# A row LSTM's three-tap filter as F(2,3) on pixel pairs, with the normalisation of x moved to GpSimd

## The chip, the cores and the metric

The kernel runs on one core of a Trainium2 chip. The metric is the time of one launch in device microseconds (us). The kernel before took 2895.79 us, the median of 3 runs (2895.6 to 2897.91). The clocks named are the mean granted clock of TensorE, with 1 as full speed.

## The reference, cut to what matters

```python
# x: (8, 96, 128, 128) float32.  GroupNorm with 32 groups, then a row LSTM, then the residual.
its = conv(gn(x), W_is * mask, taps over w)       # input part of the gates, all rows at once
def step(h, c, row):                              # 128 rows, one after the other
    ss    = conv(h, W_ss, three taps over w)      # 96 channels of h to 4*96 gate channels
    gates = ss + its[row]
    f, i, o = sigmoid(...);  g = tanh(...)
    c = f * c + i * g
    h = o * tanh(c)
    return h, c
out = x + h of every row
```

Each row needs the h of the row above, so the rows are a chain. The mask leaves two taps of the input filter (w-1 and part of w). Everything is float32.

## The kernel before

Channels lie on the partitions. The eight images are two halves of four, and one row of one half is a 512-column operand. I call the work for one row of one half a **step**; there are 2 x 128 = 256 of them, and the halves alternate, so that TensorE works on one half while ScalarE and VectorE work on the other. Four rows make a **block**, eight steps. The gates of a step are four products of 512 columns for each of three tiles of 128 gate channels. They are summed in `ps`, which the kernel places in the memory called PSUM, where all its products are written; all other tiles lie in the memory called SBUF:

```python
for a in order:                       # normalised x, channels 0-63, two taps in one product
    nc.tensor.matmul(ps[a], wt[:, 3, bass.ts(a, P)], xin[:, r, :, :], start=True, stop=False)
for a in order:
    for p in range(3):                # h at w-1, w, w+1 (taps 0 and 1 also carry x of channels 64-95)
        kk = C if p == 2 else P
        nc.tensor.matmul(ps[a], wt[0:kk, p, bass.ts(a, P)],
                         hin[0:kk, r, :, p : p + W], start=False, stop=(p == 2))
# ... (cut) tanh and sigmoid of three tiles on ScalarE; f*c, i*g, c on VectorE; tanh(c) on ScalarE
nc.vector.tensor_mul(h, sg[2], th)
nc.gpsimd.tensor_add(xr, xr, h)       # residual, in place
```

VectorE also normalises x for the block to come, one image after each step:

```python
for r in range(R):
    for s in range(NH):
        step(s, k, r)
        if k + 1 < NB:
            normalise(s, k + 1, r)    # three nc.vector.tensor_scalar(...)
```

## Time and profile before

| | before |
|---|---|
| median time | 2895.79 us |
| span of the profiled run | about 2891 us |
| TensorE busy | 2642.7 us, 91% |
| VectorE, ScalarE, GpSimd busy | 45%, 42%, 11% |
| one step | 10.32 us |

The prediction below shows the busy table, the chain, the main groups and a step of the timeline. Two more lines of the page of the kernel before matter later: the TensorE clock in 40 equal slices of the span (in tenths; 9 is 90% or more), and VectorE's larger group of normalisations (line, engine, operation, operands and shapes, count; then total busy us and mean ns; then the idle time before them).

```profile
PEclk9999999999999999999999999999999999999999
...
L163 DVE TENSOR_SCALAR x<-x,rstd,nmr 64x508 f32<-64x508 f32 (+1 forms) x512 | 327.1, 639 | 20.9 <-PE ps L185 13.7
```

The runs of this kernel have a mean clock of 0.999. These normalisations are work of VectorE that the change takes away; they lie beside TensorE's products, so they cost the kernel before nothing.

### The profile page before, as it was taken

The numbers are of one execution on the slowest core, as the hardware profiler recorded it, in microseconds if no ns is written. First come the engines' busy times: TensorE is split into PE (matmuls) and PEld (weight loads), VectorE is DVE, ScalarE is ACT, GpSimd is POOL, SyncE is SP. The second block draws the span as 40 slices with busy tenths as digits, with TensorE's granted clock in tenths as the row PEclk, the third lists the DMA queues.
The fourth block names the chain that finished last, engine by engine and source line by source line (L and its number), as shares of the span: only waits on it lengthen the run. The fifth ranks groups of instructions, "written<-read, shape, count | busy, mean of one in ns | idle before, by whom it ended". The sixth has DMA issues, their size and how long they took to land.

```text
span 2890.6 us, 18393 instructions
## 1 busy us (share of the span) xinstructions
PE 2642.7 (91%) x6148; PEld 1164.1 (40%) x6148; DVE 1313.2 (45%) x2070; ACT 1212.1 (42%) x1796; POOL 317.8 (11%) x282
## 2 busy tenths in 40 slices
PE   0007999999999999999999999999999999999998
PEld 0003444444444444444444444444444444444443
DVE  6776444443344444433444444334444443344422
ACT  0003444444444444444444444444444444444444
POOL 1000111111111111111111111111111111111111
PEclk9999999999999999999999999999999999999999
DMA  9992111001111111011111110111111101111000
GB/s 229 236 239 69 44 44 44 26 21 41 44 44 44 44 44 29 21 39 44 44 44 44 44 32 20 37 44 44 44 44 44 33 22 34 44 44 44 22 22 22
DMA packets 55597, 152.96 MB, mean 53 GB/s; under 512 B 3024, under 2 KB 3152, under 8 KB 52432
## 3 DMA queue, kind: packets, MB, share of 16 engines
q1 hardware_dynamic: 54784, 151.01, 19.8%
q10 hardware_dynamic: 720, 0.78, 0.1%
q8 instruction: 51, 0.84, 0.1%
q14 instruction: 42, 0.34, 0.0%
HBM read 101.44 MB, written 50.33 MB: 53 GB/s over the span
## 4 chain that ended last, share of the span: by engine, by line
PE 91%; DMA 6%; DVE 2%; issue 1%; ACT 0%; POOLq 0%; POOL 0%; DVEq 0%; ACTq 0%
PE ps L191 68%; PE ps L185 23%; DMA xc<-in_x_dram 6%; DVE bst L114 2%; DMA wt<-in_w_ss_dram 0%; POOLq L282 0%; POOL x L220 0%; DVE st L115 0%; DVE hb L218 0%; DVE c L214 0%; DVE ig L213 0%; ACT g L205 0%; ACT th L215 0%; PE pm L127 0%; PE pv L133 0%
## 5 line engine op out<-in xcount | busy, mean ns | idle before, releaser
L191 PE MATMUL ps<-hb,wt 128*128 128x512 f32 (+1 forms) x4608 | 2022.0, 592 | 0.0
L191 PEld LDWEIGHTS ps<-hb,wt 128*128 128x128 f32 (+1 forms) x4608 | 872.5, 189 | 1107.8 <-issue 1107.5
L205 ACT ACTIVATE g<-ps,bias 32x512 f32<-32x512 f32 x768 | 522.7, 681 | 1164.5 <-PE ps L191 1164.4
L185 PE MATMUL ps<-x,wt 128*128 128x512 f32 x1536 | 702.7, 593 | 8.1 <-issue 8.1
L212 DVE TENSOR_TENSOR fc<-sf,c 96x512 f32<-96x512 f32 x256 | 176.1, 688 | 1077.3 <-ACT sf L208 1077.3
L220 POOL TENSOR_TENSOR x<-x,hb 96x512 f32<-96x512 f32 x256 | 308.5, 1205 | 2561.2 <-DVE hb L218 2457.0
L185 PEld LDWEIGHTS ps<-x,wt 128*128 128x128 f32 x1536 | 290.8, 189 | 378.0 <-issue 377.8
L163 DVE TENSOR_SCALAR x<-x,rstd,nmr 64x508 f32<-64x508 f32 (+1 forms) x512 | 327.1, 639 | 20.9 <-PE ps L185 13.7
L213 DVE TENSOR_TENSOR ig<-si,g 96x512 f32<-96x512 f32 x256 | 176.2, 688 | 233.6 <-ACT g L205 231.7
L215 ACT ACTIVATE th<-c 96x512 f32<-96x512 f32 x256 | 161.3, 630 | 264.4 <-DVE c L214 264.4
L218 DVE TENSOR_TENSOR hb<-so,th 96x512 f32<-96x512 f32 x256 | 175.7, 686 | 161.8 <-ACT th L215 160.5
L127 PE MATMUL pm<-d,gm 96*96 96x8 f32 x2 | 0.5, 318 | 228.8 <-DVE d L125 228.8
L214 DVE TENSOR_TENSOR c<-fc,ig 96x512 f32<-96x512 f32 x256 | 175.8, 687 | 8.7
L114 DVE BATCH_NORM_STATS2 bst<-xc 96x6 f32<-96x512 f32 x256 | 154.9, 675 | 51.8 <-DMA xc<-in_x_dram 51.8
L208 ACT ACTIVATE so<-ps,bias 96x512 f32<-96x512 f32 x256 | 174.7, 683 | 6.5
L208 ACT ACTIVATE si<-ps,bias 96x512 f32<-96x512 f32 x256 | 174.7, 682 | 3.2
L208 ACT ACTIVATE sf<-ps,bias 96x512 f32<-96x512 f32 x256 | 174.6, 682 | 3.1
L163 DVE TENSOR_SCALAR hb<-x,rstd,nmr 32x512 f32<-32x512 f32 x256 | 124.1, 540 | 1.3
L135 ACT ACTIVATE t<-v 96x8 f32<-96x8 f32 x1 | 0.2, 208 | 225.1 <-DVE v L134 225.1
L127 PEld LDWEIGHTS pm<-d,gm 96*96 96x96 f32 x2 | 0.4, 256 | 228.8 <-DVE d L125 228.8
L115 DVE BATCH_NORM_AGGREGATE st<-bst 96x2 f32<-96x192 f32 x8 | 8.1, 1018 | 0.3
L102 POOL MEMSET hb<- 128x2080 f32 x4 | 7.3, 1830 | 0.0
(27 smaller groups left out, 10.2 us busy)
## 6 DMA issues: line engine op xcount, KB each, us to landing
xc<-in_x_dram SPq DMA_DIRECT2D x32, 1536.0 KB, 15.2
x<-in_x_dram SPq DMA_DIRECT2D x64, 768.0 KB, 5.0
out_dram<-x SPq DMA_DIRECT2D x64, 768.0 KB, 4.3
wt<-in_w_ss_dram ACTq DMA_DIRECT2D x1, 432.0 KB, 11.4
wt<-in_w_is_dram ACTq DMA_DIRECT2D x3, 96.0 KB, 11.1
gm<-in_gmat_dram ACTq DMA_DIRECT2D x1, 36.0 KB, 9.5
bias<-in_b_ss_dram ACTq DMA_DIRECT2D x1, 1.5 KB, 10.2
bias<-in_b_is_dram ACTq DMA_DIRECT2D x1, 1.5 KB, 9.8
```

What stands on the lines that cost most here:

```text
L114: nc.vector.bn_stats(bst[:, k * (CH // SN) + j, :], xc[:, bass.ts(j, SN)])
L163: nc.vector.tensor_scalar(dst, t[lo:hi, j, :, 0:w], rstd[lo:hi, b : b + 1], nmr[lo:hi, b : b + 1], ALU.mult, ALU.add,)
L185: nc.tensor.matmul(ps[a], wt[:, 3, bass.ts(a, P)], xin[:, r, :, :], start=True, stop=False)
L191: nc.tensor.matmul(ps[a], wt[0:kk, p, bass.ts(a, P)], hin[0:kk, r, :, p : p + W], start=False, stop=(p == 2),)
L205: nc.scalar.activation(g[a * 32 : (a + 1) * 32], ps[a][C:P], AF.Tanh, bias=bias[C:P, a : a + 1])
L208: nc.scalar.activation(sg[a], ps[a][0:C], AF.Sigmoid, bias=bias[0:C, a : a + 1])
L212: nc.vector.tensor_mul(fc, sg[0], c)
L213: nc.vector.tensor_mul(ig, sg[1], g)
L214: nc.vector.tensor_add(c, fc, ig)
L215: nc.scalar.activation(th, c, AF.Tanh)
L218: nc.vector.tensor_mul(h, sg[2], th)
L220: nc.gpsimd.tensor_add(xr, xr, h)
```

## The change

**Intent.** Take a pair of neighbouring pixels and the four values of h that their three taps touch, d0 to d3. With the filter F(2,3) the two outputs need four products in place of six:

```text
m1 = (d1+d2) * (w0+w1+w2)/2      m2 = (d2-d1) * (w0-w1+w2)/2      (the signs are the kernel's)
first output  = m1 + m2 + (d0-d2) * w0
second output = m1 - m2 + (d3-d1) * w2
```

In the cut below, `mm(a, half, w, operand)` is one product with filter `w` into half 0, half 1 or (None) both halves of tile `a`. The weights are combined once. Per step VectorE makes the sum and the difference of h (`vs`, `vf`), and GpSimd makes the other differences (`vd`). TensorE makes m1 and m2 of each tile. ScalarE copies m1 (adding the bias), VectorE writes m1+m2 and m1-m2 back into the same PSUM, and TensorE accumulates the rest on top. Products of h are now 256 columns wide. The normalisation goes to GpSimd, because VectorE has more to do. The part of x in channels 64 to 95 is shared with the products of h, so GpSimd makes its sums and differences too.

```diff
-        for a in order:
-            nc.tensor.matmul(ps[a], wt[:, 3, ...], xin[:, r, :, :], start=True, stop=False)
-        for a in order:
-            for p in range(3):
-                nc.tensor.matmul(ps[a], wt[0:kk, p, ...], hin[0:kk, r, :, p : p + W], ...)
+        for a in order:
+            mm(a, 0, 1, vs[s][i][:, r].rearrange(flat), start=True)
+            mm(a, 1, 2, vf[s][i][:, r].rearrange(flat))
+            m1 = gt(f"m{a}", (P, HB))
+            lo, hi = ps[a][:, 0:HB], ps[a][:, HB : 2 * HB]
+            nc.scalar.activation(m1, lo, AF.Identity, bias=bias[:, a : a + 1])
+            nc.vector.tensor_add(lo, m1, hi)
+            nc.vector.tensor_sub(hi, m1, hi)
+        for a in order:
+            mm(a, None, 4, xn[s][i][:, r].rearrange("p t b j -> p (t b j)"))
+            mm(a, 0, 0, vd[s][i][:, r, 1, :, 0:J])
+            mm(a, 1, 3, vd[s][i][:, r, 0, :, 0:J], stop=True)
 ... (cut: gates and cell state as before, without the bias)
+            nc.vector.tensor_add(vs[s][n][0:C, rn], e, o)
+            nc.vector.tensor_sub(vf[s][n][0:C, rn], o, e)
+            nc.gpsimd.tensor_sub(vd[s][n][0:C, rn, :, :, 0:J], strided(h...), h3)
-        nc.gpsimd.tensor_add(xr, xr, h)
+        nc.gpsimd.tensor_add(xr_, xr_, h3)
 ... (cut)
+    with tc.manual_schedule(engines={mybir.EngineType.Pool}):      # GpSimd keeps the order written
+        for k in range(NB):
 ...
+                    step(s, k, r)
+                    if k + 1 < NB:
+                        normalise_own(s, k + 1, r)               # GpSimd: tensor_scalar, memset
+                        if r > 0:
+                            normalise_shared(s, k + 1, r - 1)    # GpSimd: tensor_scalar, two sums
+                        if r == R - 1:
+                            normalise_shared(s, k + 1, r)
```

## The prediction

Terms are cut from the text below; the sums stand as my estimates:

- **VectorE.** The source of the 0.42 us of a 256-column operation is cut. A straight line between two sizes in the kernel before (163 ns for 8 columns, 687 for 512) gives 0.42 us too.
- **GpSimd.** Cut are its time for a normalisation and what rests on it: the term of the shared part of an image and the 8 us before the first product (249 + 8 = 257). The last row of a block came to 6.9 us with the cut terms; the terms that still stand (1.18 + 1.18 + 0.12) are 2.48 of it. The block wait in the 2635 and the 2876 us, and so the 2768, rests on this sum.
- **Contention.** What stands is the measured row (1.51 us), and the chances of 55% and 45%, which were my guess.

> **What bounds the kernel now.** I read the busy table first, then the chain of work that ended last, then the groups of instructions, and last the timeline of one step (a step is one image row of one batch half; there are 2 x 128 = 256).
>
> ```profile
> PE 2642.7 (91%) x6148; PEld 1164.1 (40%) x6148; DVE 1313.2 (45%) x2070; ACT 1212.1 (42%) x1796; POOL 317.8 (11%) x282
> PE 91%; DMA 6%; DVE 2%; issue 1%; ACT 0%; POOLq 0%; POOL 0%; DVEq 0%; ACTq 0%
> L191 PE MATMUL ps<-hb,wt 128*128 128x512 f32 (+1 forms) x4608 | 2022.0, 592 | 0.0
> L205 ACT ACTIVATE g<-ps,bias 32x512 f32<-32x512 f32 x768 | 522.7, 681 | 1164.5 <-PE ps L191 1164.4
> L185 PE MATMUL ps<-x,wt 128*128 128x512 f32 x1536 | 702.7, 593 | 8.1 <-issue 8.1
> L212 DVE TENSOR_TENSOR fc<-sf,c 96x512 f32<-96x512 f32 x256 | 176.1, 688 | 1077.3 <-ACT sf L208 1077.3
> L220 POOL TENSOR_TENSOR x<-x,hb 96x512 f32<-96x512 f32 x256 | 308.5, 1205 | 2561.2 <-DVE hb L218 2457.0
> ```
>
> The chain is 91% TensorE, and the matmul group L191 has 0.0 us of idle time ahead of it: the row loop is TensorE-bound without a gap. ScalarE and VectorE idle because they wait for matmuls, so their time is hidden. 6144 matmul instructions in 256 steps are 24 a step: each of the program's 12 float32 products is two instructions. The timeline shows the period and the handoffs:
>
> ```profile
> 1508.72 2.74 PE L185 MATMUL ps<-x,wt 128*128 128x512 f32 x6
> 1508.72 0.19 PEld L185 LDWEIGHTS ps<-x,wt 128*128 128x128 f32 x1 [0.24 <-issue]
> 1508.92 0.68 ACT L205 ACTIVATE g<-ps,bias 32x512 f32<-32x512 f32 x1 [1.20 <-PE ps L191]
> 1509.63 0.69 DVE L213 TENSOR_TENSOR ig<-si,g 96x512 f32<-96x512 f32 x1 [1.19 <-ACT g L205]
> 1511.14 0.63 ACT L215 ACTIVATE th<-c 96x512 f32<-96x512 f32 x1 [0.83 <-DVE c L214]
> 1511.87 0.69 DVE L218 TENSOR_TENSOR hb<-so,th 96x512 f32<-96x512 f32 x1 [0.82 <-ACT th L215]
> ...
> 1519.04 2.74 PE L185 MATMUL ps<-x,wt 128*128 128x512 f32 x6
> ```
>
> A step lasts 1519.04 - 1508.72 = 10.32 us, or 0.43 us an instruction. The next half's matmuls start at 1508.72 and this half's last tanh at 1508.92, so TensorE to ScalarE costs 0.20 us after the slot; ScalarE to VectorE about 0.03, VectorE to ScalarE 0.09, to GpSimd 0.07. 256 x 10.32 = 2642 of the 2891 us span: about 249 us are statistics, start and end.
>
> One more pair of rows matters, a normalisation (VectorE) meeting the residual add (GpSimd):
>
> ```profile
> 259.77 1.51 DVE L163 TENSOR_SCALAR hb<-x,rstd,nmr 32x512 f32<-32x512 f32 x1
> 259.82 1.18 POOL L220 TENSOR_TENSOR x<-x,hb 96x512 f32<-96x512 f32 x1 [244.19 <-DVE hb L218]
> ```
>
> This normalisation takes 0.54 us elsewhere. Here it ends 0.28 us after the GpSimd add ended (261.00): it was held for the whole add.
>
> [...]
>
> **The change part by part.**
>
> *TensorE.* A step has 15 products: three of 512 columns and twelve of 256. That is 6 x 0.43 + 24 x 0.215 = 7.74 us, three quarters of 10.32. A 0.19 us weight load still fits a 0.215 us slot, narrowly. Were TensorE the only bound: 256 x 7.74 = 1981, plus about 257 (the old 249[...]) = 2238 us.
>
> *VectorE.* Removed: (327.1+124.1)/256 = 1.76 us of normalisation a step. Added: six 256-column sums into PSUM and two for h, 8 x 0.42 = 3.4. Total 2.75 + 3.4 = 6.1 us. *ScalarE.* Three 256-column copies with bias; 0.68 less 256 columns at (681-208)/504 ns (the 8-column root took 208) is about 0.45 to 0.47. Total 4.7 + 1.4 = 6.1 us. *GpSimd.* Per step: a difference 1.18 and the residual add 1.18,[...] a memset 0.12[...]; but the last row of a four-row block has two shared parts, 6.9 us. *DMA* reads the rows about 2.3 times, roughly 117 MB beside 50 MB of stores over 2000 us: hidden.
>
> None of these sums exceeds 7.74; what counts is the new path inside a step. TensorE makes the sums and differences products of all gate tiles (2.58 us), then must wait until ScalarE and VectorE have written m1+m2 and m1-m2 back into PSUM. By the instruction order of the built program, each engine does that after work of the other half. With 0 at the end of the previous step's matmul slots: ScalarE tanh 0.20-0.88, sigmoid to 1.56, copies to 2.03 and 2.50, tanh(c) to 3.13, third copy to 3.60. VectorE i*g 0.91-1.60, c to 2.33, two sums and a difference, overlapping a little, to 3.48. So TensorE, done with its first part at 2.58, resumes at 3.56: 1 us lost. Its second part, 5.16 us, ends at 8.72, if VectorE's remaining h (3.41-4.10), difference, two sums of h, sum and difference (to about 5.9) stay ahead of the third tile's start at 7.0. They do without contention. **8.72 x 256 + 257 = 2489 us.**
>
> *Block boundary.* The first matmul of a new block waits for GpSimd's last shared part. Its queue for that step starts when h is done, 4.1 after the step's own matmuls, and lasts 6.9, to 11.0; TensorE does the other half's step meanwhile and wants it at 8.72. Some 2.3 us are lost, twice in 8 steps (both halves): 0.57 a step, 9.29 x 256 + 257 = **2635 us**.
>
> [...] h ends at 4.10, GpSimd's difference runs 4.17-5.35, and VectorE's two sums of h (two SBUF inputs) stand in the queue ahead of the third tile's PSUM sums. If the first waits to 5.35 (ends 5.63), then GpSimd's residual add goes first (to 6.67), then the second sum (6.95), the third tile is ready at 7.8 and TensorE starts it at 7.9 instead of 7.0: a step of 9.62. The boundary wait, with GpSimd held in turn by VectorE, is about 2.5: 9.62 + 0.61 = 10.23, and 256 x 10.23 + 257 = **2876 us**.
>
> **The rivals.** (A) TensorE stays the bound, about 2240 us: speaks for it that every engine's sum is below 7.74; against it the dependence ScalarE to VectorE to TensorE in mid-step, which two alternating halves cannot hide because the engines take the halves in turn. (B) GpSimd's block end and the mid-step wait, no real contention: about 2635. (C) Full exclusion[...]: about 2876, level with before; for it the 1.51 us row[...], against it [...]that two queued VectorE sums may pass together. (D) GpSimd is worse than estimated (interleaved pixels, normalisation 0.9 us) with full exclusion: each boundary wait grows by 1 to 2 us, about 3000.
>
> **Range and chances.** I give full exclusion 55% and the rest 45%: 0.55 x 2876 + 0.45 x 2635 = 2768 us. The range 2570 to 2970 spans from just above the contention-free path to most of D. Faster by 2% means under 2838: nearly all of B, a fifth to a quarter of C's spread: 0.57. Within 2%: 0.26. Slower: 0.17.
>
> **What would show it right or wrong.** In the profile after, TensorE's slots should be about 0.215 us for 256 columns[...]. The matmul of the interleaved x should carry an idle of about 1 us in each step, ended by VectorE; the third tile's should too if the lock is real, and then sums of h take 1 to 1.3 us rather than 0.42. The first matmul of each block should wait 2 to 3 us for GpSimd. GpSimd rows: [...]adds near 1.2. The prediction fails low if VectorE and GpSimd overlap freely and blocks join smoothly, and high if GpSimd's strided work is slow enough to bound each step, or if gaps lower TensorE's granted clock, which is full in all slices before.

## The result, and the profile after

The changed kernel took 2945.64 us, the median of 4 runs (2938.35 to 2952.89); the kernel before took 2895.78 us in the same rounds. The ratio is 1.0172, with a 95% interval of 1.0155 to 1.0190. A ratio is the mean time of one kernel's fast runs over that of the other's fast runs of the same rounds, so it is not quite the ratio of the medians. By the limit of 2% this is "the same", on the slower side. The profiled run spans 2936.5 us at a mean clock of 0.958.

First the page of the changed kernel: its busy table and the engines' shares of the chain that ended last.

```profile
PE 2255.3 (77%) x7688; PEld 1481.7 (50%) x7688; DVE 2074.1 (71%) x3352; ACT 1364.6 (46%) x2564; POOL 1567.7 (53%) x1828
...
DVE 46%; PE 21%; POOL 18%; DMA 5%; ACT 5%; issue 4%; ACTq 0%; POOLq 0%; DVEq 0%
```

No engine is busy for more than 77%. TensorE's share of the chain fell from 91% to 21%; VectorE and GpSimd now carry 64%. The chain goes through three of them, so this kernel is bound by handoffs. The change also loads more of x (HBM read 185.73 MB, 101.44 before), but DMA is on the chain only with the loads for the statistics at the start, 5% of it.

Next the groups of the same page, in the columns explained above.

```profile
L246 PE MATMUL ps<-xn,wt 128*128 128x512 f32 x1536 | 842.1, 630 | 250.7 <-DVE ps L260 249.4
L246 PE MATMUL ps<-vs,wt 128*128 128x256 f32 x1536 | 522.5, 425 | 212.0 <-POOL vs L231 212.0
L259 DVE TENSOR_TENSOR ps<-m,ps 128x256 f32<-128x256 f32 x768 | 309.4, 422 | 274.1 <-ACT m L258 274.1
L287 DVE TENSOR_TENSOR vf<-hh 96x256 f32<-96x256 f32 x254 | 380.7, 1499 | 0.0
L286 DVE TENSOR_TENSOR vs<-hh 96x256 f32<-96x256 f32 x254 | 294.0, 1157 | 0.0
L288 POOL TENSOR_TENSOR vd<-hh 96x512 f32<-96x512 f32 x254 | 263.7, 1038 | 1082.3 <-DVE hh L279 1082.3
L294 POOL TENSOR_TENSOR x<-x,hh 96x512 f32<-96x512 f32 x256 | 377.3, 1474 | 14.1 <-DVE hh L279 14.1
L198 POOL TENSOR_SCALAR xn<-xr,rstd,nmr 128x512 f32<-128x512 f32 x256 | 247.8, 968 | 199.0 <-DVE nmr L176 198.9
L198 POOL TENSOR_SCALAR vd<-x,rstd,nmr 32x512 f32<-32x512 f32 x256 | 235.5, 920 | 23.4
L231 POOL TENSOR_TENSOR vs<-vd 32x256 f32<-32x256 f32 x256 | 247.5, 967 | 21.3
```

Read three things here. TensorE's idle time stands before the products of `xn` (it waits for VectorE's write-back into `ps`) and before the products of `vs` (it waits for GpSimd). The write-back itself, a 256-column VectorE operation into PSUM, takes 422 ns; the sums of h, `vs` and `vf`, are as many columns and take 1157 and 1499 ns. And each of GpSimd's operations shown takes 0.92 us or more, the normalisations 0.92 to 0.97.

The timeline of the changed kernel shows both waits and a third thing (start in us, duration, engine, line, operation, operands; in brackets the idle time before it and what ended it).

```profile
1500.00 1.04 POOL L288 TENSOR_TENSOR vd<-hh 96x512 f32<-96x512 f32 x1 [5.07 <-DVE hh L279]
1500.17 1.15 DVE L286 TENSOR_TENSOR vs<-hh 96x256 f32<-96x256 f32 x1
1501.00 1.47 POOL L294 TENSOR_TENSOR x<-x,hh 96x512 f32<-96x512 f32 x1
1501.24 1.51 DVE L287 TENSOR_TENSOR vf<-hh 96x256 f32<-96x256 f32 x1
...
1503.12 0.43 DVE L260 TENSOR_TENSOR ps<-m,ps 128x256 f32<-128x256 f32 x1
1503.60 1.13 PE L246 MATMUL ps<-xn,wt 128*128 128x512 f32 x2 [0.51 <-DVE ps L260]
...
1508.72 1.22 PE L246 MATMUL ps<-vs,wt 128*128 128x256 f32 x2 [3.12 <-POOL vs L231]
...
1510.58 1.06 PE L246 MATMUL ps<-vs,wt 128*128 128x256 f32 x2
...
1519.97 0.59 PE L246 MATMUL ps<-vs,wt 128*128 128x256 f32 x2
```

- **The lock.** GpSimd's difference ends at 1500.00 + 1.04 = 1501.04, and VectorE's sum `vs` ends at 1501.32, 0.28 us later. GpSimd's residual add ends at 1502.47, and `vf` ends at 1502.75, again 0.28 us later; over all steps the medians of both are 0.28. I call this the lock: the sum, whose two inputs are both in SBUF, ends only after the GpSimd operation beside it. The write-back of the third tile stands behind them in VectorE's queue, and TensorE waits for it at 1503.60.
- **The block's end.** The first product of a new block waits 3.12 us for the last shared sums of GpSimd.
- **The clock.** After that wait the same pair of products takes 1.06 us where it takes 0.59 later. From start to start, an instruction of 256 columns takes 0.427 us instead of 0.216. Half the clock lasts for about the first ten instructions of a step (in the clock records 3.4 us, or 6.8 in 13 of 57 stretches).

I sorted the steps by their row in the block (start of the first product to start of the next step's first product, medians):

| step of the block | period before, us | period after, us |
|---|---|---|
| row 0, first half | 10.32 | 14.36 |
| row 0, second half | 10.32 | 11.10 |
| rows 1, 2 and row 3, first half | 10.32 | 9.36 |
| row 3, second half | 10.32 | 12.65 |

A regular step of 9.36 us is 7.76 us of product slots, 0.82 us at the wait for the write-back (a slot of 0.934 in place of 0.216, and 0.10 in the next one) and 0.78 us at the wait for the third tile (0.90, and again 0.10). By the means (14.16, 10.85 and 12.67) a block of eight steps takes 84.5 us, which is 8 x 9.36 = 74.9 and about 9.7 at the boundary: twice 3.3 us of waiting and twice about 1.5 us of half clock.

So the account closes: 224 us before the first product of a row and 10 after the last one, 256 x 7.76 = 1987 us of slots, 256 x 1.60 = 410 us of waits in the steps, and 31 x 9.7 = 300 us at the block boundaries give 2931 us; the span is 2936.5. The change saved 256 x (10.32 - 7.76) = 655 us of TensorE's slots and spent 710 us on waits.

### The profile page after: what moved, and what is told of

Its sections match the earlier page's. It is cut to its first block, busy times and chain, and to the rows that moved or that the text cites. A ratio compares the mean times of both kernels' runs of the same rounds, so it can differ in the third digit from the quotient of the medians.

```text
span 2936.5 us, 26168 instructions
## 1 busy us (share of the span) xinstructions
PE 2255.3 (77%) x7688; PEld 1481.7 (50%) x7688; DVE 2074.1 (71%) x3352; ACT 1364.6 (46%) x2564; POOL 1567.7 (53%) x1828
## 3 DMA queue, kind: packets, MB, share of 16 engines
q10 hardware_dynamic: 1040, 1.18, 0.2%
q8 instruction: 63, 1.03, 0.1%
HBM read 185.73 MB, written 50.33 MB: 80 GB/s over the span
## 4 chain that ended last, share of the span: by engine, by line
DVE 46%; PE 21%; POOL 18%; DMA 5%; ACT 5%; issue 4%; ACTq 0%; POOLq 0%; DVEq 0%
PE ps L246 21%; DVE vf L287 9%; DVE ps L259 8%; DVE vs L286 7%; DVE ps L260 6%; DVE hh L279 6%; DMA xc<-in_x_dram 5%; POOL vd L198 5%; DVE g L273 4%; DVE c L274 4%; POOL vs L231 4%; ACT g L269 4%; POOL x L294 3%; POOL xn L198 2%; POOL vd L288 2%
## 5 line engine op out<-in xcount | busy, mean ns | idle before, releaser
L246 PE MATMUL ps<-xn,wt 128*128 128x512 f32 x1536 | 842.1, 630 | 250.7 <-DVE ps L260 249.4
L269 ACT ACTIVATE g<-ps 32x512 f32<-32x512 f32 x768 | 454.2, 591 | 953.2 <-PE ps L246 953.1
L246 PEld LDWEIGHTS ps<-vd,wt 128*128 128x128 f32 x3072 | 582.2, 190 | 411.7 <-issue 370.6
L246 PE MATMUL ps<-vd,wt 128*128 128x256 f32 x3072 | 788.2, 378 | 0.0
L246 PE MATMUL ps<-vs,wt 128*128 128x256 f32 x1536 | 522.5, 425 | 212.0 <-POOL vs L231 212.0
L258 ACT ACTIVATE m<-ps,bias 128x256 f32<-128x256 f32 x768 | 358.0, 466 | 386.6 <-PE ps L246 385.8
L246 PE MATMUL ps<-vf,wt 128*128 128x256 f32 x1536 | 517.6, 422 | 0.0
L259 DVE TENSOR_TENSOR ps<-m,ps 128x256 f32<-128x256 f32 x768 | 309.4, 422 | 274.1 <-ACT m L258 274.1
L294 POOL TENSOR_TENSOR x<-x,hh 96x512 f32<-96x512 f32 x256 | 377.3, 1474 | 14.1 <-DVE hh L279 14.1
L287 DVE TENSOR_TENSOR vf<-hh 96x256 f32<-96x256 f32 x254 | 380.7, 1499 | 0.0
L260 DVE TENSOR_TENSOR ps<-m,ps 128x256 f32<-128x256 f32 x768 | 325.4, 424 | 8.9
L286 DVE TENSOR_TENSOR vs<-hh 96x256 f32<-96x256 f32 x254 | 294.0, 1157 | 0.0
```

The costliest lines, as they stand in the source:

```text
L246: nc.tensor.matmul(o, wt[:, p, bass.ts(a, P)], rhs, start=start, stop=stop, skip_group_check=True)
L258: nc.scalar.activation(m1, lo, AF.Identity, bias=bias[:, a : a + 1])
L259: nc.vector.tensor_add(lo, m1, hi)
L260: nc.vector.tensor_sub(hi, m1, hi)
L269: nc.scalar.activation(g[a * 32 : (a + 1) * 32], ps[a][C:P], AF.Tanh)
L286: nc.vector.tensor_add(vs[s][n][0:C, rn], e, o)
```

## The experiments

The theory: the gain is real and is eaten by (1) a write-back in mid-step, (2) VectorE's sums of h, held while GpSimd reads SBUF, and (3) GpSimd's queue at the block's end, with (4) half a clock after it. The main rivals: the sums are slow for another reason; the waits merely follow from GpSimd being too slow as a whole; the clock costs nothing by itself. All eleven kernels were run in three rounds beside the kernel before, and all results are right except where it is said. The runs were made in three sessions; the kernel before took 2895.6 to 2896.4 us in each. The runs show the lock (a 256-column sum in 1.16 and 1.50 us where 0.41 is its time alone), not what makes it.

| run | median us | ratio to before [95%] | clock |
|---|---|---|---|
| changed kernel | 2945.64 | 1.0172 [1.0155, 1.0190] | 0.958 |
| e10_write_only (wrong) | 2835.80 | 0.9798 [0.9782, 0.9815] | 0.963 |
| e1_vd_after_vf | 2909.51 | 1.0048 [1.0033, 1.0063] | 0.943 |
| e2_early_shared | 2726.08 | 0.9414 [0.9398, 0.9430] | 0.998 |
| e4_warm | 2805.16 | 0.9684 [0.9670, 0.9699] | 0.998 |
| e3_both | 2563.79 | 0.8854 [0.8841, 0.8867] | 0.998 |
| e6_no_writeback (wrong) | 2555.87 | 0.8829 [0.8816, 0.8843] | 0.965 |
| e5_norm_on_dve | 3029.67 | 1.0463 [1.0443, 1.0483] | 0.974 |
| e8_act_norm | 2963.85 | 1.0237 [1.0222, 1.0252] | 0.980 |
| e7_pipelined | 2591.00 | 0.8947 [0.8932, 0.8962] | 0.964 |
| e9_pipelined_act | 2367.12 | 0.8173 [0.8161, 0.8185] | 0.999 |
| e11_split_norm | 2355.58 | 0.8135 [0.8123, 0.8147] | 0.999 |

### e10_write_only: does GpSimd's reading hold VectorE's sums?

GpSimd's two operations beside the sums are replaced by memsets of similar length, which read nothing. The result is wrong (relative error 1.0), since the differences and the residual are missing.

```diff
-            nc.gpsimd.tensor_sub(vd[s][n][0:C, rn, :, :, 0:J], strided(h...), h3)
+            nc.gpsimd.tensor_copy(tick, h[:, 0, 0, 0:1])
+            for _ in range(2):
+                nc.gpsimd.memset(vd[s][n][0:C, rn, :, :, 0:J], 0.0)
-        nc.gpsimd.tensor_add(xr_, xr_, h3)
+        for _ in range(3):
+            nc.gpsimd.memset(xr_, 0.0)
```

Expected: 

> Wrong results on purpose: GpSimd's difference (1.04 us) and residual add (1.47 us), which run beside VectorE's two sums of h, become two and three memsets of the same place and about the same time, begun by a one-column copy of h. Theory (it is GpSimd's reading of SBUF that holds VectorE[...]): the sums fall from 1.16 and 1.50 to about 0.42 us, the third tile's idle goes, undisturbed steps last about 8.6 us, and as GpSimd starts no later than before, the block wait stays near 3 us: about 2760, 2720 to 2820 us. Rival (any GpSimd instruction holds VectorE, or the sums are slow for their strided rows): sums stay at 1.1 to 1.5 us, 2900 us or more.

Measured: 2835.80 us, a little above the expected range. The timeline of this run:

```profile
1508.47 1.10 POOL L291 MEMSET vd<- 96x512 f32 x2
1508.55 0.41 DVE L287 TENSOR_TENSOR vs<-hh 96x256 f32<-96x256 f32 x1
...
1508.88 0.41 DVE L288 TENSOR_TENSOR vf<-hh 96x256 f32<-96x256 f32 x1
```

Both sums run wholly inside GpSimd's memsets and take 0.41 us. So neither the layout of h nor the mere presence of GpSimd's work makes them slow: it is GpSimd's **reading**. The steps of row 1, with no shared part behind them, fall from 9.36 to 8.58 us, the 0.78 us of the third tile. In the other rows the shared normalisation and sums, which still read, hold VectorE's later operations (c takes 989 ns), and the steps of row 2 and of row 3's first half stay at 9.18 us. One of the two block waits grew from 3.3 to 4.3 us. These two, about 31 x 3 x 0.6 = 56 us and 31 us, are more than the run was over its range.

### e1_vd_after_vf: take the lock away in the right kernel

A one-column copy makes GpSimd wait for the second sum before it starts its difference.

```diff
             nc.vector.tensor_sub(vf[s][n][0:C, rn], o, e)
+            nc.gpsimd.tensor_copy(tick, vf[s][n][0:C, rn, 0, 0:1])
             nc.gpsimd.tensor_sub(
```

Expected: 

> One GpSimd copy of a single column of vf, ahead of GpSimd's difference, makes GpSimd start only after both of VectorE's sums of h. Theory ([...]each sum of h waits out a whole GpSimd instruction): the sums fall from 1.16 and 1.50 us to about 0.42 each, the idle of TensorE ahead of the third tile (0.90 us start to start where 0.22 is a slot) goes, an undisturbed step falls from 9.36 to about 8.65 us, and GpSimd, starting about 1.2 us later, makes the wait at a block's start longer by under 1 us: about 2800 us in all, 2760 to 2840. Rival (the write-back in mid-step alone costs the time[...]): 2945 us or more, as nothing but a wait is added.

Measured: 2909.51 us. The mechanism was right and the expected time was not. The groups of sums and, below, the view of waits (total us, times, longest) of this run:

```profile
L288 DVE TENSOR_TENSOR vf<-hh 96x256 f32<-96x256 f32 x254 | 104.9, 413 | 0.0
L287 DVE TENSOR_TENSOR vs<-hh 96x256 f32<-96x256 f32 x254 | 104.8, 413 | 0.0
```

```profile
PE ps L247 <- POOL vs L232: 313.0, 64, 14.1
```

The sums fell to 0.413 us, the gap at the third tile is gone, and a step of row 1 takes 8.58 us. But GpSimd now starts later in every step, and TensorE's wait at the block boundary grew from 212.0 to 313.0 us. The steps of rows 2 and 3 fell only to 9.0 us, since GpSimd's shared parts now meet i*g and c (769 and 931 ns, where the changed kernel had 689 and 809). Of about 0.78 us a step, 200 us in all, only 36 us arrived: the rest was given back, 100 us of it in this one line of waits.

### e2_early_shared: take the block wait away

The shared images are normalised in rows 1 and 2 (two in each), not after rows 1, 2 and 3 (one, one and two).

```diff
-                        if r > 0:
-                            normalise_shared(s, k + 1, r - 1)
-                        if r == R - 1:
-                            normalise_shared(s, k + 1, r)
+                        if r in (1, 2):
+                            normalise_shared(s, k + 1, 2 * r - 2)
+                            normalise_shared(s, k + 1, 2 * r - 1)
```

Expected: 

> The shared normalisation of the next block is done in rows 1 and 2 (two images each), none in row 3. Theory (a block's first matmul waits for GpSimd's last shared part, and the wait also lowers TensorE's clock): all steps last about 9.36 us, the 9.7 us that a block loses at its start (two waits of 3.3 and about 3.1 of slow matmuls) go, about 2640 us. Rival (GpSimd is simply overloaded: two shared parts in a step make 8.8 us of its work[...]): the waits only move to rows 1 and 2, 2800 us or more.

Measured: 2726.08 us, clock 0.998, between the two expectations. The waits and one group of VectorE in this run:

```profile
PE ps L246 <- POOL vs L231: 18.5, 2, 14.1
```

```profile
L274 DVE TENSOR_TENSOR c<-sf,g 96x512 f32<-96x512 f32 x256 | 239.4, 935 | 8.8
```

The boundary wait went from 64 times to 2, and the half clock with it: the steps of row 0 take 9.36 us. The 300 us of the boundary would have been saved whole, but the shared parts now overlap VectorE's cell-state operations of rows 2 and 3: c takes 935 ns (809 in the changed kernel, and 689 is the time of i*g there), and those four steps of a block take 10.0 us instead of 9.36. 31 x 4 x 0.64 = 79 us go back, and 300 - 79 = 221; the gain measured is 220. In this trace c takes 1.19 us in four steps of a block and 0.69 in the other four. That it is the reading of GpSimd that holds c is argued from e10_write_only, not tested alone.

### e4_warm: what does half the clock cost?

Four products into a spare PSUM tile keep TensorE busy during the block wait; nothing reads them.

```diff
+        if k > 0 and r == 0:
+            for _ in range(4):
+                nc.tensor.matmul(junk, wt[:, 4, 0:P], wt[:, 4, :], start=True, stop=True, ...)
         for a in order:
             mm(a, 0, 1, vs[s][i][:, r].rearrange(flat), start=True)
```

Expected: 

> Four dummy products (384 columns, to a spare PSUM bank, about 2.6 us) are put on TensorE ahead of the first product of each block, where it waits 3.3 us for GpSimd anyhow. Results stay right. Theory (the long wait drops TensorE's clock to half, so that 24 slots after it take 0.43 instead of 0.22 us): the slots stay at 0.22 us, about 3 us a block are saved, 2945 - 31 x 3.1 = about 2850 us, and the granted clock rises from 0.958 to about 1. Rival (the slots are slow for another cause, such as weight loads or the data's lateness): 2945 us, clock unchanged.

Measured: 2805.16 us, clock 0.998. TensorE's timeline at a boundary in this run:

```profile
1512.44 2.74 PE L256 MATMUL junk<-wt 128*128 128x384 f32 x8
1515.74 0.70 PE L247 MATMUL ps<-vs,wt 128*128 128x256 f32 x2 [0.56 <-POOL vs L232]
...
1516.96 0.59 PE L247 MATMUL ps<-vs,wt 128*128 128x256 f32 x2
...
1524.68 2.74 PE L256 MATMUL junk<-wt 128*128 128x384 f32 x8
1527.26 0.60 PE L247 MATMUL ps<-vs,wt 128*128 128x256 f32 x2
```

At the first half (the first two lines) the wait for GpSimd is as long as before (1512.44 + 2.74 + 0.56 = 1515.74: about 3.3 us), but the pairs after it take 0.59 us and not 1.06. The block takes 80.15 us instead of 84.54 on average: 31 x 4.39 = 136 us. The clock is thus a cost of its own: its 3.1 us a block. The other 1.3 us came at the second half (the last two lines): there nothing waits for GpSimd any more, whose last sum ended 1.5 us before the products start. The filler itself takes 1527.26 - 1524.68 = 2.58 us where the wait took 3.3, and is longer than was needed; nor does the third tile wait in the step before it. Why GpSimd is earlier there I did not test. The run came out 45 us under what I expected. Useless work made the kernel 4.8% faster.

### e3_both: e1 and e2 together

The edit is that of e1_vd_after_vf and that of e2_early_shared.

Expected: 

> Both of the edits above. If they are independent causes, the gains add: a step of about 8.65 us throughout, 8.65 x 256 + 240 = about 2455 us. If GpSimd becomes the bound in rows 1 and 2 (8.3 to 8.8 us of work a step), 2500 to 2600.

Measured: 2563.79 us. Alone the two edits saved 36 and 220 us, 256 in sum; together they saved 382. The lock's gain could not arrive while the block wait took it back. The time lies in the second of the expected ranges, but not for the reason given there: GpSimd, with as much work as in the changed kernel, has 1% of the chain (TensorE 54%, VectorE 30%), so it was not too slow as a whole. Steps take 8.58 us in row 1, about 9.1 in row 2 and 9.6 in row 3. This is already 11.5% faster than the kernel before.

### e6_no_writeback: what is the mid-step wait worth?

This is e3_both without the copies and sums back into PSUM, and with the bias in the gate activations; wrong (relative error 0.067).

```diff
-            m1 = gt(f"m{a}", (P, HB))
-            lo, hi = ps[a][:, 0:HB], ps[a][:, HB : 2 * HB]
-            nc.scalar.activation(m1, lo, AF.Identity, bias=bias[:, a : a + 1])
-            nc.vector.tensor_add(lo, m1, hi)
-            nc.vector.tensor_sub(hi, m1, hi)
```

Expected: 

> Wrong results on purpose: the third of the combined kernel's costs taken alone. On top of the two edits (early shared parts, sums of h ahead of GpSimd) ScalarE's copies and VectorE's sums into PSUM are left out, the second products accumulate on the bare first ones. Theory (what is left above TensorE's 7.76 us a step is the wait for the write-back in mid-step): 7.8 to 8.0 us a step, 2240 to 2320 us. Rival (the remaining time is GpSimd's[...]): 2450 to 2560 us.

Measured: 2555.87 us, 236 us over the range that I expected and within the rival's (what remains is GpSimd's). Undisturbed steps take 7.75 us, so the write-back is the cause of the 0.82 us. But the total hardly moved from e3_both. TensorE's waits in this run:

```profile
PE ps L247 <- POOL xn L218: 145.4, 31, 5.4
PE ps L247 <- POOL vd L285: 78.7, 31, 2.6
```

At every block TensorE now runs into GpSimd's normalisation and difference, and waits up to 5.4 us; the half clock is back with these waits (0.965, where e3_both has 0.998). GpSimd has 53% of the chain. So with the steps faster, GpSimd's queue sets the time (its normalisations take 0.97 and 1.08 us here, where the changed kernel has 0.80 before the row loop). That a block takes 72.40 us, so near the 72.55 of e3_both, I can't explain; it may be chance.

### e5_norm_on_dve and e8_act_norm: move the normalisation off GpSimd

Each is a change of the one helper, to VectorE and to ScalarE; the scheduler places the work.

```diff
     def norm(dst, src, lo, layout, b):
-        nc.gpsimd.tensor_scalar(
+        nc.vector.tensor_scalar(                  # e5_norm_on_dve
+        nc.scalar.activation(dst, src, AF.Identity, bias=nmr..., scale=rstd...)   # e8_act_norm
```

Expected of e5_norm_on_dve: 

> One part of the change undone: x is normalised on VectorE again, all else (F(2,3), the shared sums on GpSimd) stays. If GpSimd's queue at the block's end is what the normalisation costs, its work in row 3 falls by about 2.8 us (0.97 and twice 0.92), the two waits of 3.3 us nearly go and with them the slow clock: 2945 - 31 x 9 = about 2670 us, less what VectorE's 1.2 us more a step cost: 2680 to 2800. Rival (VectorE has no room, which is why the change moved it): VectorE, 6.1 us plus 2 us of waits[...], becomes the bound: 2945 or more.

Expected of e8_act_norm: 

> The changed kernel with one edit: x normalised on ScalarE (an activation with scale and bias for each image) in place of GpSimd; order of the rest as the scheduler has it. Theory: GpSimd's work in row 3 falls from about 9.4 to 6 us, the waits at a block's start and the slow clock nearly go, other steps stay at 9.36 us: 9.36 x 256 + 250 = about 2650 us, up to 2780 if ScalarE's strict order holds up gates as VectorE's did in the run before. Rival (the block wait is not GpSimd's queue): 2900 us or more.

Measured: 3029.67 and 2963.85 us, both **slower** than the kernel before; both expectations missed; the numbers lie in the rivals' ranges. VectorE's waits in e5_norm_on_dve, and then the timeline of TensorE and ScalarE in e8_act_norm:

```profile
DVE vd L198 <- POOL vf L232: 152.3, 192, 1.4
```

```profile
1503.79 1.03 PE L245 MATMUL ps<-vd,wt 128*128 128x256 f32 x4
...
1505.29 1.63 ACT L198 ACTIVATE xn<-xr,nmr,rstd 128x512 f32<-128x512 f32 x2
1506.94 0.59 ACT L268 ACTIVATE g<-ps 32x512 f32<-32x512 f32 x1
```

In e5_norm_on_dve the block wait is nearly gone (it occurs once), but VectorE's normalisation stands between the sum and the difference of the third tile's write-back, and waits there 192 times for GpSimd's shared sums; most steps take about 11.1 us. In e8_act_norm the block wait for the shared sums is gone too, so the rival's reason (that it was not GpSimd's queue) did not hold. But two normalisations of 0.82 us each run ahead of a gate that other engines wait for: its last product had ended at 1503.79 + 1.03 = 1504.82, and it starts at 1506.94, when both are done. TensorE's longest wait for the write-back is 2.7 us (0.8 in the changed kernel). Work that has slack, put ahead of work that has none, cost its whole length here. For e5_norm_on_dve I did not separate the order from the lock (`vf` takes 1.51 us there).

### e7_pipelined: set the order by hand

All four engines keep a written order. The last gate of the previous step and the first write-back of the current one are interleaved, each tile's write-back is a pair, and the sums of h come after the third tile's write-back. The shared parts lie in rows 1 and 2 as in e2_early_shared.

```diff
+        cur.first();  prev.tanh(2);  cur.copy(1);  prev.sigmoid(2);  prev.ig()
+        cur.back(1);  cur.copy(0);   prev.cell();  cur.back(0);      cur.copy(2)
+        prev.hidden();  cur.back(2)
+        prev.spread()                     # vs, vf on VectorE; vd and the residual on GpSimd
+        prev.ahead();  cur.second()       # normalisations; the rest of the products
+        ... (cut: tanh and sigmoid of tiles 1 and 0, then f*c)
```

Expected: 

> Same arithmetic as the changed kernel, but with the order of all four engines set by hand: the other half's first copy and write-back go between this half's last tanh and sigmoid, VectorE finishes a tile's pair before it goes on, and the sums of h come after the third tile's pair, so that a wait[...] is off the path; shared parts early as before; no extra GpSimd copy. Theory: [...]a step of 7.8 to 8.3 us, 2260 to 2380 us. Rival[...]: 8.5 to 9 us a step, 2430 to 2560 us.

Measured: 2591.00 us: far from my range, and 31 us over the rival's too. The engines' shares of the chain, and TensorE's longest wait in the loop:

```profile
POOL 53%; PE 31%; DMA 6%; DVE 5%; issue 3%; ACT 1%; POOLq 0%; ACTq 0%; DVEq 0%
```

```profile
PE ps L249 <- POOL xn L217: 179.7, 31, 5.9
```

Undisturbed steps take 7.85 us, so the order removes both waits inside the step without removing the lock: the sums of h are still held (`vf` takes 1.03 us on average), but nobody waits for them. GpSimd has become the bound, as the rival said: 53% of the chain, and a wait of up to 5.9 us at each block, with the half clock after it (0.964).

### e9_pipelined_act: the same order, and the normalisation placed by hand on ScalarE

```diff
     def norm(dst, src, lo, layout, b):
-        nc.gpsimd.tensor_scalar(...)
+        nc.scalar.activation(dst, src, AF.Identity, bias=nmr..., scale=rstd...)
 ...
+        prev.own()                        # after the last sigmoid, ahead of tanh(c)
+        prev.shared();  prev.sums()       # after tile 1's gates; images (), (0), (1, 2), (3) by row
```

Expected: 

> The kernel with the hand-set order, and x normalised on ScalarE (one activation with scale and bias for each image) in place of GpSimd. Theory: [...]a step is TensorE's 7.76 us with little on top, 2240 to 2300 us. Rival (ScalarE, 5.6 + 1.2 us a step and in strict order, becomes the bound or holds up tanh of c): 2350 us or more, worse than the one before.

Measured: 2367.12 us, clock 0.999: 18.3% less than before, though 67 us over the range that I expected. The busy table and the group of `vf` in this run:

```profile
PE 2065.9 (87%) x7688; PEld 1427.9 (60%) x7688; DVE 2039.1 (86%) x3352; ACT 1763.5 (75%) x3076; POOL 1064.6 (45%) x1316
...
L324 DVE TENSOR_TENSOR vf<-hh 96x256 f32<-96x256 f32 x254 | 384.1, 1512 | 0.0
```

This is 224 us less than e7_pipelined, with the move that lost time under the scheduler's order in e8_act_norm. The edit does more than that move: the shared images lie in rows 1, 2 and 3 (one, two and one), and GpSimd's shared sums come later in the order. The runs do not part these. `vf` still takes 1.51 us, and TensorE does not wait for it. Steps take 8.27 us in row 0, 7.85 in row 1, 8.08 in row 2 and 8.9 in row 3.

### e11_split_norm: one image's shared normalisation back on GpSimd

```diff
             s * BH + j,
+            pool=j == 2 and k > 0,        # nc.gpsimd.tensor_scalar for this image
```

Expected: 

> The fastest kernel so far with one of the four shared images normalised on GpSimd instead of ScalarE, so that no step has two of them on ScalarE. Row 3's steps last 8.9 us there against 7.85 in row 1, because ScalarE with two shared parts (8.1 us) is over a step. Theory: row 3 falls to about 8.1 us, 1.6 us a block, 2367 - 50 = about 2315 us. Rival (GpSimd's reading, not ScalarE, is what slows row 3): 2367 us or more.

Measured: 2355.58 us, the best version: 18.7% less than before. TensorE's groups in this run:

```profile
L263 PE MATMUL ps<-xn,wt 128*128 128x512 f32 x1536 | 809.8, 609 | 16.6 <-DVE ps L287 12.9
...
L263 PE MATMUL ps<-vs,wt 128*128 128x256 f32 x1536 | 464.6, 384 | 24.8 <-POOL vs L245 24.6
```

The idle times before `xn` and `vs` are 16.6 and 24.8 us, where the changed kernel had 250.7 and 212.0. Row 3's first half fell from 8.9 to 8.05 us as expected, but its second half did not (8.97 and 8.87), and GpSimd's longer queue gave 0.57 us back at the start of each block (8.27 became 8.84); so the run came out some 40 us over what I expected.

One alternative remains untested: a write-back in which VectorE takes m1 and m2 both from PSUM, without ScalarE's copy.

## Why the prediction was right or wrong

The range held (2570 to 2970) and the direction did not: I gave 57% to "faster", and the kernel is 1.7% slower. A range of 400 us that takes in both directions holds easily.

**Right.** TensorE's slots are 0.216 us (said: about 0.215), and weight loads fit (0.190 to 0.213 us each). The wait in mid-step for the write-back is there, with the cause named; e6_no_writeback removes it and gets 7.75 us steps. It is 0.82 us where I said 1. The gap at the third tile and the sums of h at 1 to 1.3 us were given as the sign of the lock, and came (1.16 us, and 1.50, which is over it); e10_write_only and e1_vd_after_vf show that the lock is the cause. Case C's regular step, 9.62 us, was 9.36.

**The step that failed first: "I give full exclusion 55% and the rest 45%".** That weighting pulled the time from 2876 down to 2768 us, and made "faster" the likelier side. There is hardly a partial case in the trace: the medians of 254 sums each are 1144 and 1514 ns, against 413 ns in the run without the lock. The trace before has no such sum beside a GpSimd operation: GpSimd's add overlaps only normalisations there, 91 times, and holds them (1.31 us in the median where 0.54 is their time alone), so the 45% for sums that are not held was my guess. The argument that two queued sums "may pass together" fell: GpSimd's residual add gets in between them each time.

**The term that was mis-sized: the block boundary.** I had 2.5 us twice a block (31 x 5.0 = 155 us). It was 9.7 us a block, 300 us. The wait itself is 3.3 us each. GpSimd's queue for the last row was given 6.9 us; its parts by the mean rows are 1.04 + 1.47 + 0.97 + 0.10 + 2 x (0.92 + 0.97 + 0.74) = 8.84 us, because a normalisation takes 0.92 to 0.97 us and the sums 0.97 and 0.74, more than the terms I had for them. Part of this is again the lock, from GpSimd's side: where no VectorE operation on SBUF overlaps them, the normalisations take 0.80 us and the sums 0.64 and 0.73. The other 1.5 us each is half a clock, which I named only as a way to fail ("if gaps lower TensorE's granted clock"); e4_warm took it away, and 136 us with it, some 31 x 3.1 = 96 of them by the clock itself.

From case C to the span: 2876 less 256 x 0.26 = 67 for the shorter step, plus 145 for the boundary, less 23 for start and end (234, not 257) is 2931, against a span of 2936.5. So case C was the right picture, with its boundary at half size; case D's long normalisation was true as well. Three slips in the working changed nothing: the loop loads 134 MB by the page's list of transfers and not 117; 2.5 us twice in eight steps is 0.63 and not 0.61; and from tanh(c) to h the timeline shown has 0.10 us from ScalarE to VectorE, not 0.03.

**What the prediction did not see** is that these costs are not a sum. Taking away the lock alone gave back most of its gain (e1), taking away lock and block wait gave more than both apart (e3), and taking away the write-back on top gave nothing (e6), until GpSimd had less to do and the order was set by hand (e9, e11). Rival A, "TensorE stays the bound", about 2240 us, is what e11_split_norm comes near: it is 5% above it.

## What to carry to other kernels

When a change takes work from the bound engine and adds short handoffs among the others, sum up not only each engine's time but the queue of each engine, in the order that the program has it, between one deadline and the next, and what two of them do to each other where they overlap (here sums of 0.41 us became 1.16 and 1.50 us beside GpSimd's reading). A wait of some 3 us at every block had two prices here, itself and the slow clock after it, and removing one wait of several told little about what all of them cost. Work with slack belongs, by hand if need be, behind the work the bound engine waits for: the same move of the normalisation to ScalarE cost 18 us in the scheduler's order (2945.64 to 2963.85) and won 224 us, with the images spread anew, in the order set by hand (2591.00 to 2367.12).

## What the traces show beyond the forecast

- **The lock.** A two-input VectorE sum is held by a GpSimd subtraction or add, which read SBUF (1157 and 1499 ns in the changed kernel), and not by a memset (0.41 us in e10_write_only). The held 256-column sum ends 0.28 us after the GpSimd operation (medians of 254), so it is held to the end of it; a free one takes 0.41 us in all. GpSimd is held in turn, by less: the residual add takes 1.47 us in the changed kernel, and 1.30 in e1_vd_after_vf, where no VectorE sum of h overlaps it.
- **GpSimd's normalisation.** For 512 columns it took 0.80 us before the row loop, with VectorE not yet in the way, and 0.92 to 0.97 us on average over the changed kernel.
- **The clock.** By the clock records of the changed kernel, half the clock came beside starts of products 3.5 us apart (57 stretches, 63 such gaps, the first of them 4.5 us): each stretch began between 1.05 us before and 1.64 us after the product that ends the gap. Shorter waits did not settle it: in e5_norm_on_dve TensorE's longest wait for the write-back was 2.1 us, and the clock was still 0.974; in e3_both it was 1.6 us, and the clock was 0.998. Filler products kept the clock up where the wait itself stayed: e4_warm has 0.998 instead of 0.958.
- **PSUM and SBUF.** A 256-column sum with one input and the output in PSUM took 0.422 us, and one wholly in SBUF, free of the lock, 0.413 us: only 9 ns apart.
